# A four-layer graph network on one core: neighbour sums as DVE reduces, bias on POOL, residual on DVE, other orders, constant tiles on PE

## The chip, the cores and the metric

The kernel runs on one core of one Trainium2 chip. Its engines are PE (matrix multiply), DVE (vector), ACT (scalar and activation functions), POOL (here mainly the engine that issues indirect DMAs) and SP (plain DMAs); each runs its own stream in order, and they meet over semaphores. The metric is device time in microseconds (us) for one execution; the kernel before has a median of 1075.28 us over three runs (1071.92 to 1076.54).

## The reference

3327 nodes with 512 features each pass through four layers over one sparse adjacency matrix (int32, 3327 x 3327, each entry one with probability 0.0012, so about four neighbours a node). Each layer takes h = relu(layernorm(x)) and adds its result to x:

```python
# layer 0: mean over the neighbours, two linear maps, relu
deg = sum(mask); agg = mask @ h / max(deg, 1)
x = x + relu(concat([h @ W_self + b_self, agg @ W_nb + b_nb]) @ W_comb + b_comb)
# layers 1 (8 heads x 64), 2 (4 heads x 128, quaternion weights), 3 (1 head x 512)
Wh = h @ W
e = leaky_relu(f_src[n] + f_dst[m]); attn = softmax over the neighbours m of e
x = x + attn @ Wh            # layer 2: x + elu(attn @ Wh)
```

Only neighbours matter, so the sums over the matrix are sums over short lists.

## The kernel before

**Tiles, slots and units.** Nodes are sorted by their number of neighbours and cut into 26 tiles of 128. A tile has as many slots as its longest list: tile 0 has 14, tile 1 eight, tiles 2 and 3 seven, 4 to 6 six, 7 to 10 five, 11 to 15 four, 16 to 20 three, 21 to 23 two, 24 and 25 one: 117 slots. `ROWS` says how many nodes have a neighbour in each slot, in steps of 32; a tile's last slots can hold 96, 64 or 32 rows. One slot is one indirect DMA by POOL (L1562), which gathers one table row of some 2 KB per node into a ring of `RING` = 33 slots of 2080 bytes per partition. A unit is one tile or a pair of tiles worked together; `ORDERS` gives the units of each layer.

**Preparation.** The adjacency is loaded and turned into lists; x is normalised; folded weights are built; `keep_y` copies the own part of layer 0 (h times the own weights) from PSUM next to the node's x. Then `scatter` (L1435) writes 26 tiles of nodes' rows to their sorted places in DRAM, 26 indirect DMAs on POOL in the order `SEQUENCE`. `back` (L1451) reads the lists and degrees of all nodes back with one DMA on SP that waits for all scatters; `degrees` (L1505) turns them into `rdeg`, one over the degree. SP then loads x and own part of each tile (`xy`, L1854).

**Layer 0.** Per tile: gathers, a cast of the lists to integers (L1862), the sum over slots, x and output. PE sums most slots by multiplying with the identity into a PSUM tile `acc` (`sum_on_pe`, L1593); then DVE scales by `rdeg` and adds the own part (L1871), adds the bias (L1879), adds min(S//2, 5) further slots one at a time, each scaled (L1887), and makes the new x with relu and residual (L1895). `project` prepares the next layer's table: DVE statistics (L1649, L1650), ACT's logarithm and exponential for the inverse deviation (L822, L824) with small DVE operations (L831 to L836), ACT normalises (L1676), PE transposes into `pt` (L1694), ACT copies (L1705), PE multiplies by the weights into `pw` (L1780, L1737 for layer 3), ACT copies to `t` (L1803), and SP stores to the table (L1822).

**Layers 1 to 3.** `attend`: gathers; scores and softmax on DVE with the exponential on ACT (L1941 to L1978); products of rows and weights in place in the ring, some slots on ACT (L2096, as many as `ON_ACT` says), the others on DVE (L2110); sums on PE (L1593), in layer 1 also on DVE one slot at a time (L2138). Then the residual (L2148 in layer 1; an ELU, L2164 to L2178, in layer 2) and `project`. Layer 3 multiplies by its weights after the sum: the first slot on ACT (L2028), the others on DVE (L2030), transposes (L2046), copies (L2052), one identity matmul that puts the residual into `pw` (L2058) and four with the weights (L2060), a copy to `t` (L2067) and an indirect DMA on POOL that scatters the tile to the output (L2072).

**What sets the order.** Within the layers, `Plan` simulates the engines: each operation has a cost, a rank (layer, unit), what it waits for, and buffers that it takes and gives (`limits`: two `acc`, two `pt`, two `pw` and so on). The engines' streams are issued in the order of the simulated starts; the plan's times are not kept, only its order. Between layers, a small memset on POOL (`mark`, L2194) waits for the table stores, and the next layer's gathers stand behind it.

Of the kernel before, what the change touches and what calls it, by code (L numbers as in the profile page):

```python
# [8 lines left out]
F32 = mybir.dt.float32  # L9
# [9 lines left out]
P = 128  # L19
# [7 lines left out]
def general_path(  # L27
# [519 lines left out]
    def l3_finish(pc, i, o):  # L547
# [16 lines left out]
ROWS = (3328, 3072, 2592, 1984, 1344, 832, 448, 224, 128, 64, 32, 32, 32, 32, 0, 0)  # L564
CAPS = tuple(-(-r // 128) for r in ROWS)
SEG = 4
RING = 33
NEVER = -1.0e30
# [4 lines left out]
    0: {S: min(S // 2, 5) for S in range(1, SLOTS + 1)},  # L573
    1: {S: min(S // 2, 5) for S in range(1, SLOTS + 1)},
    2: {S: 0 for S in range(1, SLOTS + 1)},
# [4 lines left out]
        (24,), (12, 21), (11,), (6,), (18,), (17,), (15,), (4,), (3,), (20,), (5, 9), (22,), (10, 19), (1,),  # L580
        (2,), (14,), (0,), (23,), (8,), (13, 16), (7,), (25,),
    ),
    1: (
        (18, 21), (22, 24), (15,), (5,), (10, 20), (2,), (17,), (12, 23), (19,), (4,), (9, 14), (7,), (11, 16),
        (8, 13), (6,), (1,), (0,), (3,), (25,),
    ),
    2: (
        (18, 23), (19, 24), (16,), (20,), (6, 11), (10, 14), (7, 12), (5, 13), (9,), (1,), (21, 22), (4,), (0,),
        (8,), (2,), (3,), (15,), (17,), (25,),
    ),  # L590
    3: (
        (0,), (7,), (17,), (15, 20), (25,), (11,), (3,), (23,), (1, 5), (24,), (4, 14), (16,), (12, 22), (8,),
        (9,), (10,), (18,), (2,), (13,), (19,), (21,), (6,),
# [4 lines left out]
    1: {S: min(S // 3, 1) for S in range(1, SLOTS + 1)},  # L598
    2: {S: S // 5 for S in range(1, SLOTS + 1)},
}  # L600

SUMMED = {1: False, 2: False, 3: False}
# [11 lines left out]
class Plan:  # L614
# [35 lines left out]
    def run(self):  # L650
        free = {}
        stock = {tag: [0.0] * n for tag, n in self.limits.items()}
        waiting = {}
        for op in self.ops:
            if not op["need"]:
                waiting.setdefault(op["engine"], []).append(op)
        order = []
        while any(waiting.values()):
            best = None
            for engine, ops in waiting.items():  # L660
                for op in ops:
                    at = max(op["ready"], free.get(engine, 0.0))
                    for tag in op["take"]:
                        at = max(at, min(stock[tag])) if stock[tag] else None
                        if at is None:
                            break
                    if at is not None and (best is None or (at, op["rank"]) < best[:2]):
                        best = (at, op["rank"], op)
            at, _, op = best
            waiting[op["engine"]].remove(op)  # L670
            for tag in op["take"]:
                stock[tag].remove(min(stock[tag]))
            op["at"] = at
            end = at + op["cost"]
            free[op["engine"]] = end
            for tag in op["give"]:
                stock[tag].append(end + 0.1)
            for after in op["next"]:
                lag = op["lag"] + (0.1 if after["engine"] != op["engine"] else 0.0)
                after["ready"] = max(after["ready"], end + lag)  # L680
                after["need"] -= 1
                if not after["need"]:
                    waiting.setdefault(after["engine"], []).append(after)
            order.append((at, len(order), op))
        assert len(order) == len(self.ops)
        for _, _, op in sorted(order, key=lambda o: o[:2]):
            if op["emit"]:
                op["emit"]()
        return max(free.values())
# [3 lines left out]
def gnn_stack_kernel(  # L693
# [41 lines left out]
    with ExitStack() as st:  # L735
# [116 lines left out]
        with tc.tile_pool(name="p0", bufs=1) as pa, tc.tile_pool(name="p0p", bufs=2, space=PSUM) as pp:  # L852
# [444 lines left out]
            for p0 in range(0, NK, 2):  # L1297
# [25 lines left out]
                for j, i in enumerate(unit):  # L1323
# [51 lines left out]
                    own_done[i] = put("act", 0.62, late_rank, keep_y, (), [y], give=("py",))  # L1375
# [74 lines left out]
            def back():  # L1450
                ins = nc.sync.dma_start(srec_f, own.rearrange("(k p) w -> p k w", p=P)[:, :, 2 * D :])  # L1451
                for other in scattered:
                    tc.add_manual_dep(
                        ins.ins,
                        other.ins.name,
                        mybir.DependencyInfo(mybir.DependencyClass.Sync, mybir.DependencyReason.DATA),
                        reason="every row is read",
                    )
# [57 lines left out]
        with tc.tile_pool(name="run", bufs=1, reuse_waits="tile") as pr, tc.tile_pool(  # L1516
# [7 lines left out]
            limits = {"xy": 3, "acc": 2, "pt": 2, "pw": 2, "h": 3, "hT": 3, "t": 3, "neg": 2, "ee": 2, "y": 3}  # L1524
# [20 lines left out]
            def gather(layer, i, rank, barrier):  # L1545
# [8 lines left out]
                for s in range(S):  # L1554
# [16 lines left out]
                    landed.append(plan.add("dma", 0.95 * held(i, s) / P, rank, None, [issue], lag=1.3))  # L1571
                return ring[:, r0 : r0 + S, :], landed, last

            def runs_of(i, lo, hi, most=SLOTS):

                out = []
                for s in range(lo, hi):
                    if out and held(i, s) == out[-1][2] and s - out[-1][0] < most:
                        out[-1][1] = s + 1
                    else:  # L1580
                        out.append([s, s + 1, held(i, s)])
                return out

# [262 lines left out]
            for number, unit in enumerate(ORDERS[0]):  # L1846
                rank = (0, number)
                updated = []
                for j, i in enumerate(unit):
# [15 lines left out]
                    left = S - ON_DVE[0][S]  # L1865
                    summed = sum_on_pe(key, g, list(range(left)), [[o] for o in landed], rank)
# [9 lines left out]

                    def emit(key=key):
                        acc = tiles["acc", key]
                        nc.vector.tensor_tensor(acc, acc, biasf, ALU.add)  # L1879

                    done = plan.add("dve", 0.7, rank, emit, [done])
                    for s in range(left, S):

                        def emit(i=i, key=key, g=g, s=s):
                            m = held(i, s)
                            acc = tiles["acc", key][:m, :]
                            nc.vector.scalar_tensor_tensor(  # L1887
                                acc, g[:m, s, :D], rdeg[:m, i : i + 1], acc, ALU.mult, ALU.add
                            )

                        done = plan.add("dve", 0.7, rank, emit, [done, landed[s]])
                        last.append(done)

                    def emit(j=j, i=i, key=key, unit=unit):
# [11 lines left out]
                        plan.add("dve", 0.7 + 0.1 * SUMMED[1], rank, emit, [done], take=taking(1, j), give=("acc", "xy"))  # L1906
# [4 lines left out]
            def attend(layer, number, unit, barrier):  # L1911
# [12 lines left out]
                act_of = {i: ON_ACT[layer][slots_of[i]] if layer < 3 else 0 for i in unit}  # L1924
# [67 lines left out]
                for j, i in enumerate(unit):  # L1992
# [56 lines left out]
                    if layer == 3:  # L2049
# [6 lines left out]
                        def emit(i=i, key=key):  # L2056
                            pw = new("pw", key, [P, 2, D], pp)
                            nc.tensor.matmul(pw[:, 0, :], ident, xres[:, i, :], start=True, stop=False)  # L2058
                            for c in range(DC):
                                nc.tensor.matmul(  # L2060
                                    pw[:, 0, :], tiles["hT", key][:, c, :], w3[:, c, :], start=False, stop=(c == DC - 1)
                                )

                        done = plan.add("pe", 4.6, rank, emit, [turned], take=("pw",), give=("hT",))

                        def emit(key=key):
                            nc.scalar.copy(new("t", key, [P, WIDE])[:, :D], tiles["pw", key][:, 0, :])  # L2067

                        done = plan.add("act", 0.6, rank, emit, [done], take=("t",), give=("pw",))
# [18 lines left out]
                    else:  # L2088
# [38 lines left out]
                        left = Si - ON_DVE[layer][Si]  # L2127

                        first = sorted(range(left), key=lambda s: s < act_of[i])
                        summed = sum_on_pe(key, g[i], first, [[made[s]] for s in first], rank)  # L2130
                        last[i] += summed
                        done = summed[-1]
                        for s in range(left, Si):

                            def emit(i=i, key=key, s=s, g=g):
                                m = held(i, s)
                                acc = tiles["acc", key][:m, :]
                                nc.vector.tensor_tensor(acc, g[i][:m, s, :D], acc, ALU.add)  # L2138

                            done = plan.add("dve", 0.7, rank, emit, [done, made[s]])  # L2140
                            last[i].append(done)
                    if layer == 1:

                        def emit(j=j, i=i, key=key, g=g, Si=Si):
# [9 lines left out]
                                "dve", 0.7 + 0.1 * SUMMED[2], rank, emit, [done], take=taking(2, j), give=("acc",) if Si > 1 else ()  # L2154
# [4 lines left out]
                    else:  # L2159
# [10 lines left out]
                        def emit(j=j, i=i, key=key, g=g, Si=Si):  # L2170
# [6 lines left out]
                            else:  # L2177
# [4 lines left out]
                                "dve", 1.4 + 0.1 * SUMMED[3], rank, emit, [bent], take=taking(3, j), give=("acc", "ee") if Si > 1 else ("ee",)  # L2182
# [6 lines left out]
            for layer in (1, 2, 3):  # L2189
# [15 lines left out]
                ends = []  # L2205
                for number, unit in enumerate(ORDERS[layer]):
                    ends += attend(layer, number, unit, barrier)
            with tc.manual_schedule():
                plan.run()
# [50 lines left out]
```

## Time and profile before

| what | us |
|---|---|
| median of three runs | 1075.28 |
| the profiled execution, its span | 1230.0 |
| PE busy | 901.8 |
| DVE busy | 726.6 |
| POOL busy | 610.1 |
| ACT busy | 518.2 |
| preparation (to the first gather of layer 0) | 278 |
| layers 0, 1, 2, 3 (first gather to first gather, the last to its last issue) | 240, 245, 236, 219 |

The profile is one execution with records of every instruction; it took longer than the timed runs. Busy times of different engines overlap. A line of a group names source line, engine, operation, output and input, shape and count, then busy time and mean duration, then the idle time before it and what ended it. A line of a wait names who waited, for what, the total in us, how often, and the longest. The clock is the share of full speed that PE was granted.

### The profile page before, as it was taken

The page shows a single profiled execution, that of the slowest core. Times are in us where ns is not written, and L with a number is a line of the kernel's source. Part 1 is how long each engine was busy: PE and PEld are TensorE (multiplying, and loading weights), DVE is VectorE, ACT ScalarE, POOL GpSimd, SP SyncE. Part 2 cuts the span into 40 slices and gives each one's busy share as a digit, 9 for nine tenths or more (in the row PEclk, how much of TensorE's full clock was granted, in tenths as well). Part 3 has the DMA queues.
Part 4 walks back from the last instruction along what each step waited for, and adds up shares of the span by engine and source line. Part 5 has one row for each costly group of instructions (what it writes and reads, how often), then busy time and mean ns, then how long its engine had stood idle before and what let it go on. Part 6 is the DMA issues. An engine that isn't in the chain of part 4 may idle for free. (4 is left out here: it accounts for less than half of the span.)

```text
span 1230.0 us, 11605 instructions
## 1 busy us (share of the span) xinstructions
PE 901.8 (73%) x2853; PEld 510.4 (41%) x2853; DVE 726.6 (59%) x1848; ACT 518.2 (42%) x1700; POOL 610.1 (50%) x719
## 2 busy tenths in 40 slices
PE   7599999854098889752979796539979832948865
PEld 4244444322075656531647464214435421423322
DVE  6499989204176557453869784628894815534441
ACT  4488886210043433422656553316554621312221
POOL 1064246717655550175757511766883236675661
PEclk9899999977599899966989889659896956978987
DMA  9999894958587772265666521665754345575561
GB/s 352 338 364 338 294 306 146 317 203 286 172 268 252 247 249 89 76 195 149 198 183 178 154 79 55 189 187 150 209 169 129 91 121 149 168 206 160 163 186 59
DMA packets 89910, 240.49 MB, mean 196 GB/s; under 512 B 24933, under 2 KB 26477, under 8 KB 89834
## 3 DMA queue, kind: packets, MB, share of 16 engines
q0 software_dynamic: 41600, 137.72, 38.1%
q1 hardware_dynamic: 48234, 101.96, 23.3%
q8 instruction: 24, 0.39, 0.1%
q14 instruction: 52, 0.43, 0.1%
HBM read 190.35 MB, written 49.27 MB: 195 GB/s over the span
## 5 line engine op out<-in xcount | busy, mean ns | idle before, releaser
L1562 POOL DMA_INDIRECT ring<-table,nbr x351 | 368.5, 1050 | 185.5 <-issue 80.9
L1593 PE MATMUL acc<-ring,ident 128*128 128x512 f32 (+1 forms) x494 | 266.6, 676 | 66.8 <-DVE ring L2110 24.3
L1780 PE MATMUL pw<-w,hT 128*128 128x264 f32 (+1 forms) x832 | 197.3, 394 | 18.3 <-ACT hT L1705 13.6
L1780 PEld LDWEIGHTS pw<-w,hT 128*128 128x128 f32 x832 | 161.2, 195 | 60.9 <-ACT hT L1705 20.5
L1593 PEld LDWEIGHTS acc<-ring,ident 128*128 128x128 f32 (+1 forms) x494 | 98.7, 215 | 175.1 <-issue 107.5
L1562 POOL DMA_INDIRECT ring<-table,srec x117 | 110.1, 941 | 77.8 <-issue 31.5
L2110 DVE TENSOR_TENSOR ring<-ring,w 128x2048 f32<-128x2048 f32 (+7 forms) x76 | 114.3, 1531 | 4.7 <-DVE w L1978 3.0
L2060 PE MATMUL pw<-w,hT 128*128 128x512 f32 x208 | 101.7, 634 | 13.3 <-ACT hT L2052 11.0
L1209 DVE FIND_INDEX8 fidx<-one_i,ai 128x8 uint32<-128x832 int32 x104 | 104.2, 1018 | 0.0
L1349 PE MATMUL pz_n<-wf,hT_n 128*128 128x512 f32 x208 | 95.2, 609 | 10.9 <-ACT hT_n L1342 8.4
L1705 ACT ACTIVATE hT<-pt 128x128 f32<-128x128 f32 (+1 forms) x312 | 81.8, 292 | 39.7 <-PE pt L1694 18.5
L1217 ACT ACTIVATE junk<-ai 128x1664 int8<-128x1664 int32 (+1 forms) x52 | 82.7, 1590 | 32.6 <-DMA ai<-in_adj_dram 32.2
L1694 PE MATMUL pt<-ident,h 128*128 128x128 f32 x208 | 36.5, 312 | 75.9 <-ACT h L1676 73.4
L1349 PE MATMUL py_n<-wf,hT_n 128*128 128x512 f32 x208 | 91.9, 592 | 0.0
L1803 ACT COPY t<-pw 128x512 f32<-128x512 f32 (+1 forms) x54 | 30.6, 566 | 134.0 <-PE pw L1780 43.9
L1941 DVE TENSOR_TENSOR e<-ring,fs 128x24 f32<-128x24 f32 (+25 forms) x96 | 15.2, 172 | 120.2 <-DMA ring<-table,nbr 102.0
L2060 PEld LDWEIGHTS pw<-w,hT 128*128 128x128 f32 x208 | 42.3, 207 | 73.2 <-issue 51.3
L1705 ACT ACTIVATION_READ_ACCUMULATOR hT<-pt 128x1 f32 x312 | 69.5, 223 | 0.0
L1694 PEld LDWEIGHTS pt<-ident,h 128*128 128x128 f32 x208 | 28.1, 160 | 96.3 <-ACT h L1676 81.6
L2194 POOL MEMSET mark<- 1x1 f32 x3 | 0.3, 88 | 132.7 <-DMA table<-t 132.7
L1349 PEld LDWEIGHTS pz_n<-wf,hT_n 128*128 128x128 f32 x208 | 39.8, 195 | 62.8 <-issue 49.4
L2046 PE MATMUL pt<-ident,y 128*128 128x128 f32 x96 | 16.4, 312 | 67.4 <-issue 56.8
(185 smaller groups left out, 1319.7 us busy)
## 6 DMA issues: line engine op xcount, KB each, us to landing
ai<-in_adj_dram SPq DMA_DIRECT2D x25, 832.0 KB
ai<-in_adj_dram SPq DMA_DIRECT2D x25, 831.5 KB
table<-t SPq DMA_DIRECT2D x52, 258.0 KB
xy<-own SPq DMA_DIRECT2D x26, 512.0 KB
table<-t SPq DMA_DIRECT2D x26, 260.0 KB
table<-zt_n SPq DMA_DIRECT2D x26, 256.0 KB
ring<-table,nbr POOLq DMA_INDIRECT x351
later<-in_x_dram SPq DMA_DIRECT2D x15, 256.0 KB
```

The costliest lines, as they stand in the source:

```text
L1209: nc.vector.max_index(fidx[:, i, qq * 8 : (qq + 1) * 8], one_i, ai[:, q * QW : min(cols, (q + 1) * QW)])
L1217: nc.scalar.activation(junk[:, :cols], tiles["ai", key][:, :cols], AF.Square, accum_out=sq[:, i, hf : hf + 1])
L1349: nc.tensor.matmul(pz, tiles["hT", key][:, c, :], wf[s][:, c, :], start=(c == 0), stop=(c == DC - 1))
L1562: nc.gpsimd.indirect_dma_start(out=ring[:m, r0 + s, : width[layer]], out_offset=None, in_=table[layer], in_offset=bass.IndirectOffsetOnAxi ...
L1593: nc.tensor.matmul(acc, ident[:m, :], g[:m, s, :D], start=(k == 0), stop=(k == len(slots) - 1))
L1694: nc.tensor.transpose(pt[:, c, :], h[:, c * P : (c + 1) * P], ident)
L1705: nc.scalar.activation(hT[:, c, :n], pt[:, c, :n], AF.Copy, accum_out=hsum[layer][:, i, c : c + 1])
L1780: nc.tensor.matmul(pw[:, b, :w], tiles["hT", key][:, c, :], wsb[layer][:, c, b, :w], start=(c == 0), stop=(c == DC - 1),)
L1803: nc.scalar.copy(t[:, :D].rearrange("p (b f) -> p b f", b=2)[:, lo:hi, :], pw[:, lo:hi, :HD])
L2046: nc.tensor.transpose(pt[:, c, :], tiles["y", key][:, c * P : (c + 1) * P], ident)
L2060: nc.tensor.matmul(pw[:, 0, :], tiles["hT", key][:, c, :], w3[:, c, :], start=False, stop=(c == DC - 1))
L2110: nc.vector.tensor_tensor(v, v, box["w"][:m, j, lo:hi, :].unsqueeze(3).to_broadcast([m, hi - lo, H, O]), ALU.mult,)
```

## The change

- `ROWS` is rounded up to multiples of 128, so each gather takes full tiles of 128 rows. The number of gathers stays.
- `ON_DVE` now names tiles. Those named have all their slots summed by one DVE `tensor_reduce` over the slots into `acc`; the others are summed wholly on PE. Named are 22 tiles in layer 0 (111 slots), 12 in layer 1 (66 slots), four in layer 2 (15 slots). The slot-by-slot additions on DVE are gone.
- The bias of layer 0 is added on POOL, to the own part in preparation, ahead of the scatter.
- `back` reads the records with 26 DMAs on SP, one per tile, in layer 0's order of tiles.
- `SUMMED[2]`: the sums for the normalisation between layers 1 and 2 come from the residual operation's own row sum and from a square with row sum on ACT, in place of DVE's statistics. The code for this was there.
- In layer 3 the residual is added by DVE as it writes `t`; the identity matmul and ACT's copy are gone.
- `fill`: PE multiplies a constant bf16 tile of ones, 128 x 512, into a PSUM tile `warm` that nobody reads, wherever the plan sees PE idle, 3.6 times per idle microsecond: 776 in all. `pt` has one buffer in place of two, which makes room for `warm`.
- `ORDERS` and `ON_ACT` are other; `ON_ACT` is now per tile (layer 1: 13 slots on ACT in place of 21; layer 2: 30 in place of 12). The ring starts at slot 0 in each layer, and the plan's cost of a gather's landing is a constant.

```diff
-ROWS = (3328, 3072, 2592, 1984, 1344, 832, 448, 224, 128, 64, 32, 32, 32, 32, 0, 0)
+ROWS = (3328, 3072, 2688, 2048, 1408, 896, 512, 256, 128, 128, 128, 128, 128, 128, 0, 0)
+FILL = 3.6
 ON_DVE = {
-    0: {S: min(S // 2, 5) for S in range(1, SLOTS + 1)},
-    1: {S: min(S // 2, 5) for S in range(1, SLOTS + 1)},
-    2: {S: 0 for S in range(1, SLOTS + 1)},
+    0: frozenset((0, 1, 2, 3, 4, 5, 6, 7, 8, 9, 10, 11, 12, 13, 14, 15, 16, 17, 18, 19, 20, 23,)),
+    1: frozenset((0, 2, 3, 4, 6, 7, 10, 13, 14, 16, 19, 23,)),
+    2: frozenset((3, 16, 17, 22,)),
 }
...
-    1: {S: min(S // 3, 1) for S in range(1, SLOTS + 1)},
-    2: {S: S // 5 for S in range(1, SLOTS + 1)},
+    1: (1, 1, 1, 1, 0, 0, 2, 1, 0, 1, 2, 0, 1, 1, 1, 0, 0, 0, 0, 0, 0, 0, 0, 0, 0, 0),
+    2: (5, 4, 1, 1, 0, 0, 1, 0, 1, 2, 0, 3, 1, 1, 1, 1, 1, 2, 1, 1, 0, 1, 1, 1, 0, 0),
 }
-SUMMED = {1: False, 2: False, 3: False}
+SUMMED = {1: False, 2: True, 3: False}
...
+        until = 0.0
+        for at, _, op in sorted(order, key=lambda o: o[:2]):
+            if op["engine"] == "pe" and fill:
+                for _ in range(int((at - until) * FILL)):
+                    fill()
+                until = at + op["cost"]
...
+                    o = put("act", 0.62, late_rank, keep_y, (), [y], give=("py",))
+                    def add_bias(i=i):
+                        own = node(i)[:, D : 2 * D]
+                        nc.gpsimd.tensor_tensor(own, own, biasf, ALU.add)
+                    own_done[i] = put("pool", 1.28, late_rank, add_bias, (), [o, whole])
...
-                ins = nc.sync.dma_start(srec_f, own.rearrange("(k p) w -> p k w", p=P)[:, :, 2 * D :])
+                for k in (k for unit in ORDERS[0] for k in unit):
+                    ins = nc.sync.dma_start(srec_f[:, k, :], own[k * P : (k + 1) * P, 2 * D :])
...
+            warm = pp.tile([P, DC, P], F32, tag="warm", name="warm", bufs=1)
+            def fill():
+                nc.tensor.matmul(
+                    warm, ones16, ones16.unsqueeze(1).to_broadcast([P, DC, P]), start=True, stop=True
+                )
-            limits = {"xy": 3, "acc": 2, "pt": 2, "pw": 2, ...
+            limits = {"xy": 3, "acc": 2, "pt": 1, "pw": 2, ...
...
+            def sum_on_dve(key, g, S, needs, rank):
+                def emit():
+                    nc.vector.tensor_reduce(
+                        new("acc", key, [P, D], pp), g[:, :S, :D].rearrange("p s d -> p d s"), AX.X, ALU.add
+                    )
+                return [plan.add("dve", 0.1 + 0.535 * S, rank, emit, needs, take=("acc",))]
...
-                    def emit(key=key):
-                        acc = tiles["acc", key]
-                        nc.vector.tensor_tensor(acc, acc, biasf, ALU.add)
-                    for s in range(left, S):
-                        def emit(i=i, key=key, g=g, s=s):
-                            nc.vector.scalar_tensor_tensor(
-                                acc, g[:m, s, :D], rdeg[:m, i : i + 1], acc, ALU.mult, ALU.add
-                            )
...
-                            nc.tensor.matmul(pw[:, 0, :], ident, xres[:, i, :], start=True, stop=False)
...
-                            nc.scalar.copy(new("t", key, [P, WIDE])[:, :D], tiles["pw", key][:, 0, :])
+                            nc.vector.tensor_tensor(
+                                new("t", key, [P, WIDE])[:, :D], tiles["pw", key][:, 0, :], xres[:, i, :], ALU.add
+                            )
```

## The prediction

> **What bounds the kernel now.** I read the clock and span first, then busy time by stage, then the waits of each stage, then the prices of single instructions. The stages are cut where POOL starts the first gather of a layer: preparation to 278 us, layers 0 to 3 from 278, 518, 763 and 999 us. Columns of the stage table: busy us (instructions) of PE, PEld, DVE, ACT, POOL, then clock, DMA share, GB/s.
>
> ```profile
> core 0: 1230.0 us, clock 0.855
> ...
> 278.00:518.00 240.00, 174.71 (x654) 119.23 (x654) 130.56 (x305) 78.27 (x359) 110.22 (x118) 0.88 0.64 206
> 518.00:763.00 245.00, 180.79 (x650) 121.69 (x650) 165.93 (x397) 119.27 (x539) 124.02 (x118) 0.85 0.51 149
> 763.00:999.00 236.00, 171.87 (x546) 93.58 (x546) 151.47 (x374) 109.69 (x443) 134.12 (x118) 0.78 0.53 154
> 999.00:1218.00 219.00, 140.40 (x364) 65.50 (x364) 91.37 (x252) 47.59 (x96) 135.87 (x143) 0.81 0.56 164
> ```
>
> PE is the busiest engine in layers 0 to 2, DVE is close behind it in 1 and 2. In layer 3 it is POOL: besides 136 us busy it has about 0.3 us of issue between its 143 transfers (43 us), 179 of 219 us. The waits of layer 0, then those of the whole run:
>
> ```profile
> POOL mark L2194 <- DMA table<-t: 56.1, 1, 56.1
> DVE acc L1871 <- remote: 42.5, 2, 36.1
> PE pt L1694 <- ACT h L1676: 37.6, 2, 36.6
> ...
> ACT t L1803 <- PE pw L1780: 28.9, 13, 4.8
> ```
>
> ```profile
> POOL mark L2194 <- DMA table<-t: 132.7, 3, 56.1
> ...
> DVE e L1941 <- DMA ring<-table,nbr: 102.0, 19, 20.7
> ...
> POOL out_dram L2072 <- ACT t L2067: 37.1, 10, 5.9
> ```
>
> POOL has issued its gathers long before a layer ends (it waits 133 us at the three marks), so PE, DVE and ACT set the length of layers 0 to 2. The single waits of 36.1 and 36.6 us on DVE and PE are one standstill of all three engines while POOL issues the first gathers of the layer; the timeline shows the like in layers 1 to 3 (about 18, 20 and 35 us). This execution is 1230 us long, the median is 1075.28: a ratio of 0.874. Most of the 155 us can lie in these 110 us of standstill, so I count them as unchanged. I make the sum on 1230 us and scale by 0.874.
>
> The prices that carry the rest, by shape (count | busy, mean ns | idle before):
>
> ```profile
> L1593 PE MATMUL acc<-ring,ident 128*128 128x512 f32 x472 | 254.0, 675 | 66.7 <-DVE ring L2110 24.3 <-issue 22.6 <-DMA ring<-table,srec 15.3
> ...
> L2058 PE MATMUL pw<-xres,ident 128*128 128x512 f32 x52 | 31.1, 685 | 0.3 <-ACT t L2067 0.3
> ```
>
> ```profile
> L1879 DVE TENSOR_TENSOR acc<-acc,biasf 128x512 f32<-128x512 f32 x26 | 18.1, 698 | 0.7
> ...
> L1148 DVE TENSOR_REDUCE w<-later 128x8 f32<-128x512 f32 x8 | 5.1, 667 | 0.0
> ...
> L1423 DVE TENSOR_REDUCE rank<-ai_sort 128x26 f32<-128x416 f32 x1 | 1.0, 951 | 0.0
> ...
> L1975 DVE TENSOR_REDUCE den<-ex 128x8 f32<-128x24 f32 x3 | 0.5, 159 | 0.3 <-ACT ex L1968 0.3
> ...
> L1975 DVE TENSOR_REDUCE den<-ex 128x8 f32<-128x56 f32 x2 | 0.5, 234 | 0.0
> ...
> L1975 DVE TENSOR_REDUCE den<-ex 128x8 f32<-128x112 f32 x1 | 0.3, 323 | 0.0
> ```
>
> **The price of the new sum.** The new reduce adds S slots that lie 2080 bytes apart, so neighbours in the sum are never neighbours in memory. L1148 reduces contiguous data: 667 ns for 512, about 1.05 ns an element over a fixed 0.13 us. L1975 is a strided sum like the new one. From 56 to 112 elements (7 and 14 per output) it grows by 89 ns: 1.59 ns an element over 0.145 us. With 3 per output it takes 159 ns for 24, no dearer than contiguous. L1423, 16 per output, is the dearest: (951-156)/416 = 1.91, or 2.29 with its fixed part. I take 1.59 for tiles of four slots or more, 1.05 below, and keep 1.05 and 1.91 as ends. The Trainium skill ("VectorE: DVE Perf Modes", the perf-mode tier table and the advice at its end) gives this instruction only the 1x rate and says to restructure where it is on a hot path; at that rate a slot would be about 0.54 us (an estimate), the low end here, and layer 0 would gain 28 us. The strided rows exceed it, in the direction of "SBUF — State Buffer" on 16-byte lines; no row has this stride.
>
> **Layer 0: -2 us.** DVE loses 50 multiply-adds (L1887, 50 x 0.753 = 37.6), 26 bias adds (18.1) and eight casts (1.4). It gains 22 reduces: 94 slots in tiles of four or more, 94 x 512 x 1.59 = 76.5; 17 others, 9.1; fixed 3.2; together 88.8. 130.6 becomes 162.3, with some 13 us of gaps between instructions 175. PE loses 61 of its 67 slots at 0.86 warm, 52 us: DVE becomes the bound. First multiply-add at 288 (below), 288 + 175 = 463, the same tail as now (last L1871 at 500.0 and two more to 502.2, next layer at 518.6: 16.4), plus the standstill 36.6: 516 against 518.6. At 1.05 DVE drops 26 us more: -28, and POOL's 146 us of issue is the next limit. At 1.91: +13.
>
> **Layer 1: -4 us.** DVE loses 50 adds (L2138, 34.6), the statistics for layer 2 (17.9 + 4.7) and some 1.5 of short operations. It gains 12 reduces (58 slots at 1.59: 47.2; 8 at 1.05: 4.3; fixed 1.7), 4.5 for eight slots' products from ACT, 3.0 for 19 small operations and perhaps 2.6 for the row sums: 166 becomes 171. PE has 66 slots to lose and 50 to take over: -13.8, to 167. ACT: -16 for products, +27 for 26 squares at 0.82 (row of L1676) and 0.22 to read the sum: 130. The longest engine falls from 181 to 171; half of that reaches the end, as PE and DVE wait for each other in turn. Ends -10 and +5.
>
> **Layer 2: -6 us.** 15 slots leave PE, 13 us off its 172, the longest. DVE stays (+11 for reduces, -10 for 18 slots' products), ACT rises by 23 to 133. ACT stands between PE's sum and the ELU, so I take half; ends -13 and +3.
>
> **Layer 3: -9 us.** PE loses the residual's 52 passes (0.86 warm a tile), ACT its copy (584 ns), DVE gains an add (691): each tile's chain to the output scatter is 0.75 us shorter. POOL stood 10 times for this chain, and gathers queue behind it: -7. The last unit has 3 slots for 6: -2. DVE's 18 us stand beside 128 idle us. Ends 0 and -25, if most of the 37 us of waits went.
>
> **Head: +3 us.** 26 adds of 1.28 us (row of L1131, 1278 ns) go to POOL, nine of them among the scatters that end preparation: the last waits for ACT's copy and puts +1.3 to +3.2 before the last scatter. The records' read-back (L1451) becomes 26 issues of 0.37 us on SP: 9.6 us. The first gather needs only the first and starts about 1 us earlier; but the degrees need all, and the loads of own parts queue behind on SP, so the first multiply-add comes at 288 instead of 284.8, and the reduces behind it on DVE with it. Ends +1 and +5.
>
> **Fillers: -4 us.** 776 multiplies of constants go into PE's stream where the plan sees PE idle (195, 127, 184, 270 by layer). At 0.22 to 0.43 us (nearest: 128x264 and 128x512 passes) they take 171 us or more. PE is idle 272 us in these stages now, about 162 without the standstills, and loses 101 of work: it fits, in program order, not by the clock. What they can win is the half clock: 0.78 means 104 us at half speed in layer 2. PE is no longer the sole bound, so -4; ends -14 and +15. The Trainium skill ("TensorE: Matmul & The Clock Gate", the HAM clock gate) lets the clock fall after an idle window of about 3.4 us, and by it constant work would hold it near full; the trace's 0.78 to 0.88 agrees in kind, and the sum by the page would be the -14 end.
>
> **At nothing or little.** One transpose buffer for two: the next tile's transposes wait for four copies on ACT, which four pw groups mostly cover: +1, at most +6. Full rows in all gathers: the issue price is the same and the DMA share is 0.51 to 0.64, which covers 1.7 MB more a layer: 0, at most +4. The new orders are in the terms above.
>
> **Sum.** -2 -4 -6 -9 +3 -4 +1 = -21: 1209 us, times 0.874 = 1057.
>
> **Rivals.** *The strided reduce is dearer* and makes DVE the bound of layers 0 and 1. Each 0.1 ns costs 4.8 us in layer 0 and about 1.5 in layer 1; the gain of 21 is gone at 1.92 ns. For: L1423. Against: the L1975 rows. At 2.29: 1230 - 21 + 44 = 1253, that is 1095. *It runs like contiguous data* (L1148): -28 and -10 in place of -2 and -4: 1177, 1029. *The gains turn into waits*: POOL's issue and the marks hold, layers 0 to 2 stay, layer 3 gives 4, the head takes 3: 1229, 1074. *Fillers on the path*: a quarter of 171 us in front of real work, +43 for -4: 1256, 1098; against it stand PE's idle rows.
>
> **How the numbers follow.** Forecast 0.41; dear reduce 0.22; cheap reduce 0.17; gains hidden 0.11; fillers 0.09. A measurement of this kernel tells about 0.5% (5 us) from no change. Faster takes the forecast but 0.02 and the cheap reduce, with a little of the hidden case: 0.57; same 0.10; slower 0.33. All ends together give 998 and 1120; 1012 to 1104 leaves out 2 in 10. The forecast's own range is 1040 to 1068.
>
> **What would show it.** The reduce's rows: 14 slots 11.5 us by my price, 7.7 by the cheap one. DVE busy 162 us in layer 0 with PE near 110 apart from fillers; the clock above 0.9; waits on L2072's successor below 30 us; degrees read at 285. I am wrong if the reduce is off by 0.3 ns, or if PE's waits sit behind fillers.

## The result

The changed kernel is slower: 1116.02 us (median of four; 1110.77 to 1116.54) against 1075.91, a ratio of 1.036, 95% interval [1.0326, 1.0395]. A second set of runs gave 1.0387 [1.0333, 1.0441] (e14).

The profile of before that the prediction reads spans 1230.0 us, though the executions timed with it took 1072 to 1077, and in the two sets of runs of e5 to e12 the kernel before takes about 1236 us; in all other sets it takes 1074 to 1076 and its second profile (e1) spans 1068.8, so sizes are compared within these alone.

The profiles of before (e1) and after, by stage: bounds and length, then busy us of PE, PEld, DVE, ACT and POOL, then clock, DMA share and GB/s. First before:

```profile
core 0: 1068.8 us, clock 0.901
...
265.75:450.65 184.90, 168.98 (x654) 116.20 (x654) 130.77 (x305) 78.41 (x359) 110.28 (x119) 0.96 0.80 267
450.65:653.93 203.28, 168.43 (x650) 115.43 (x650) 164.97 (x397) 118.70 (x539) 128.04 (x118) 0.94 0.62 179
653.93:865.36 211.43, 171.01 (x546) 91.63 (x546) 150.81 (x374) 110.27 (x443) 140.19 (x118) 0.81 0.59 171
865.36:1068.80 203.44, 135.46 (x364) 63.03 (x364) 91.71 (x252) 47.32 (x96) 136.75 (x143) 0.82 0.61 178
```

Then after:

```profile
core 0: 1114.7 us, clock 0.933
...
274.15:485.37 211.22, 169.13 (x731) 117.24 (x732) 171.10 (x241) 77.11 (x357) 110.74 (x118) 0.91 0.73 246
485.37:707.32 221.95, 189.50 (x748) 125.93 (x747) 173.75 (x327) 123.15 (x526) 137.44 (x118) 0.92 0.61 172
707.32:908.54 201.22, 178.02 (x703) 97.09 (x702) 149.33 (x343) 131.61 (x511) 130.91 (x118) 0.92 0.66 189
908.54:1114.70 206.16, 167.16 (x562) 75.17 (x560) 106.22 (x264) 34.77 (x70) 137.51 (x143) 0.94 0.64 184
```

Of the 46 us between the two spans, preparation has 8, layer 0 has 26, layer 1 has 19, layer 3 has 3; layer 2 gives 10 back. PE's busy time now includes 198 us of constant multiplies.

In layer 0 DVE is busy 171 of 211 us, and 168 of the 177 us from its first scaling with the degrees (289.8) to its last residual (466.8). The reduces of after, by shape (elements read; count | busy, mean ns | idle before):

```profile
L1607 DVE TENSOR_REDUCE acc<-ring 128x512 f32<-128x3584 f32 x5 | 32.9, 6588 | 0.1
...
L1607 DVE TENSOR_REDUCE acc<-ring 128x512 f32<-128x7168 f32 x2 | 26.2, 13085 | 0.1
L1607 DVE TENSOR_REDUCE acc<-ring 128x512 f32<-128x2048 f32 x7 | 25.5, 3650 | 0.0
L1607 DVE TENSOR_REDUCE acc<-ring 128x512 f32<-128x1536 f32 x9 | 17.3, 1920 | 0.0
```

From 7 to 14 slots a reduce grows by 6497 ns: 928 ns a slot, 1.81 ns an element, against 640 ns a slot in a tile of three. The waits of layer 0 say what that does:

```profile
ACT ln L828 <- DVE mv L1679: 74.2, 16, 28.5
POOL mark L2201 <- issue: 48.9, 1, 48.9
ACT h L1705 <- DVE nmr L842: 35.3, 19, 5.1
...
DVE degs L1518 <- DMA srec<-own: 25.7, 1, 25.7
```

ACT stands 74 us for a tile's statistics (40.8 in e1), since the next tiles' reduces stand before them on DVE, and POOL, with all gathers out, waits 49 us at the mark that ends the layer (34.9 in e1). DVE itself waited until 288.4 for the degrees; in e1 it had them at 265.0. Its reading of the degrees and its first scaling (start, us, engine, line), in e1:

```profile
264.95 0.18 DVE L1505 CAST degs<-srec 128x26 f32<-128x26 int32 x1 [11.15 <-DMA srec<-own]
272.82 0.76 DVE L1871 SCALAR_TENSOR_TENSOR acc<-acc,rdeg,xy 128x512 f32<-128x512 f32 x1 [1.98 <-PE acc L1593]
```

and after:

```profile
288.37 0.18 DVE L1518 CAST degs<-srec 128x26 f32<-128x26 int32 x1 [25.70 <-DMA srec<-own]
289.83 0.76 DVE L1902 SCALAR_TENSOR_TENSOR acc<-acc,rdeg,xy 128x512 f32<-128x512 f32 x1 [0.91 <-DMA xy<-own]
```

From the first scaling to the first gather of layer 1 it is 177.8 us in e1 and 195.6 after. So layer 0 ends 35 us later: 17 because its first scaling comes later, 18 because the stretch behind it is longer.

### The profile page after: what moved, and what is told of

The parts are those of the page before. It is cut to its first block, busy times and chain, and to the rows that moved or that the text cites. A ratio compares the mean times of both kernels' runs of the same rounds, so it can differ in the third digit from the quotient of the medians.

```text
span 1114.7 us, 12395 instructions
## 1 busy us (share of the span) xinstructions
PE 942.1 (85%) x3393; PEld 527.9 (47%) x3393; DVE 796.5 (71%) x1693; ACT 529.8 (48%) x1727; POOL 652.0 (58%) x745
## 5 line engine op out<-in xcount | busy, mean ns | idle before, releaser
L1582 POOL DMA_INDIRECT ring<-table,nbr x351 | 379.3, 1080 | 124.0 <-issue 82.6
L1540 PE MATMUL warm<-ones 128*128 128x512 bf16 x776 | 198.0, 400 | 0.0
L1622 PE MATMUL acc<-ring,ident 128*128 128x512 f32 x310 | 158.3, 648 | 22.2 <-DMA ring<-table,srec 12.1
L1607 DVE TENSOR_REDUCE acc<-ring 128x512 f32<-128x1536 f32 (+7 forms) x38 | 170.0, 4472 | 0.5
L1540 PEld LDWEIGHTS <-ones 128*128 128x128 bf16 x776 | 79.3, 103 | 88.2 <-issue 22.4
L2125 DVE TENSOR_TENSOR ring<-ring,w 128x2048 f32<-128x2048 f32 (+3 forms) x66 | 108.2, 1664 | 1.5
L1223 ACT ACTIVATE junk<-ai 128x1664 int8<-128x1664 int32 (+1 forms) x52 | 82.8, 1592 | 35.1 <-DMA ai<-in_adj_dram 34.9
L1622 PEld LDWEIGHTS acc<-ring,ident 128*128 128x128 f32 x310 | 58.8, 204 | 81.6 <-issue 47.0
L1355 PE MATMUL py_n<-wf,hT_n 128*128 128x512 f32 x208 | 95.3, 610 | 0.0
L1955 DVE TENSOR_TENSOR e<-ring,fs 128x16 f32<-128x16 f32 (+15 forms) x72 | 12.6, 179 | 76.0 <-DMA ring<-table,nbr 75.4
L1705 ACT ACTIVATE h<-xres,nmr,rs 128x512 f32<-128x512 f32 x52 | 41.5, 818 | 53.3 <-DVE nmr L842 35.3
```

The lines of the kernel that those rows point to most:

```text
L1223: nc.scalar.activation(junk[:, :cols], tiles["ai", key][:, :cols], AF.Square, accum_out=sq[:, i, hf : hf + 1])
L1355: nc.tensor.matmul(pz, tiles["hT", key][:, c, :], wf[s][:, c, :], start=(c == 0), stop=(c == DC - 1))
L1540: nc.tensor.matmul(warm, ones16, ones16.unsqueeze(1).to_broadcast([P, DC, P]), start=True, stop=True)
L1582: nc.gpsimd.indirect_dma_start(out=ring[:m, r0 + s, : width[layer]], out_offset=None, in_=table[layer], in_offset=bass.IndirectOffsetOnAxi ...
L1607: nc.vector.tensor_reduce(new("acc", key, [P, D], pp), g[:, :S, :D].rearrange("p s d -> p d s"), AX.X, ALU.add)
L1622: nc.tensor.matmul(acc, ident[:m, :], g[:m, s, :D], start=(k == 0), stop=(k == len(slots) - 1))
```

## The experiments

Layer lengths in us, from the profiles of the sets in which the kernel before takes 1074 to 1076 (stages cut as above):

| kernel | median | prep. | L0 | L1 | L2 | L3 |
|---|---|---|---|---|---|---|
| before (e1) | 1072.3 | 265.8 | 184.9 | 203.3 | 211.4 | 203.4 |
| after | 1116.0 | 274.1 | 211.2 | 222.0 | 201.2 | 206.2 |
| e2, after without constant multiplies | 1125.6 | 272.1 | 212.4 | 223.0 | 202.8 | 215.7 |
| e3, after with the old split of sums | 1091.2 | 269.9 | 192.4 | 219.1 | 201.7 | 207.8 |
| e4, after with pair additions | 1089.5 | 274.8 | 190.5 | 218.5 | 196.7 | 207.9 |
| e13, before with the reduces alone | 1165.1 | 266.5 | 222.8 | 234.3 | 226.6 | 208.6 |
| e14, after again | 1120.1 | 270.8 | 211.2 | 224.3 | 204.0 | 206.9 |
| e15, before with layer 2's order and ACT slots | 1068.7 | 266.0 | 184.5 | 204.8 | 203.1 | 202.6 |
| e16, e15 with weights in PSUM | 1077.8 | 267.3 | 189.4 | 212.4 | 198.3 | 202.9 |
| e17, before with one transpose buffer | 1093.4 | 268.8 | 190.0 | 215.7 | 218.3 | 203.4 |
| e18, e15 with more ACT slots in layer 1 | 1079.4 | 265.4 | 183.7 | 217.8 | 203.4 | 205.2 |

A profiled span differs from the median of its kernel by up to 8 us, and preparation by up to 5 us between profiles that share it.

**e1, the kernel before again.**

> The kernel before, unchanged, for a second profile of it. Both theories: 1076 us, no difference. Theory of the profiling artefact: the standstills of 18 to 37 us at the start of each layer belong to the first profiled execution, not to the kernel; a second profile then has a span near 1075 us and layers of about 200 us. If they belong to the kernel, the span is near 1230 again.

1072.34 us, ratio 0.9987 [0.9955, 1.0019], span 1068.8. PE, DVE and ACT are idle together for 5, 9, 10.5 and 26 us of layers 0 to 3, against 48, 25, 25 and 37 in the first profile: most of the standstills are not the kernel's, save in layer 3. What is left in each layer is one run of gathers and a tail. POOL issues layer 0's 117 gathers in 145.5 us without one wait, layer 1's in 163.3, layer 2's in 175.4, and layer 3's in 176.6, with the output scatters and 13.1 us of waits for their tile between them. Behind its last gather it waits 34.9, 35.8 and 35.2 us at the marks (the tail, below), and layer 3 lasts another 26.8. So POOL's issue is the longest single stretch of every layer, which the first profile hid. PE is still the busiest engine (169 of 185 us in layer 0).

**e2, no constant multiplies.**

```diff
-                plan.run(fill)
+                plan.run()
```

> The changed kernel without the 776 constant multiplies on PE. Theory 1 (the strided sums on DVE, 0.93 us a slot, bound layers 0 and 1): 1105 to 1125 us against 1116, since DVE stays saturated; PE's clock falls from 0.93. Theory 2 (the constant multiplies stand in front of real work on PE): 1085 us or less.

1125.57 us, 1.0512 [1.0478, 1.0546], at the upper end of theory 1 and 5 to 10 us slower than with them (1116 and, in e14, 1120), and the clock falls from 0.933 to 0.864. Theory 2 is out: the constant multiplies help. Nearly all of it is in layer 3 (215.7 against 206.2), where the clock goes from 0.94 to 0.80; layers 0 to 2 differ by 1 to 2 us.

**e3, the old split of the sums.**

```diff
-                    if i in ON_DVE[0]:
-                        summed = sum_on_dve(key, g, S, landed, rank)
-                    else:
-                        summed = sum_on_pe(key, g, list(range(S)), ...)
+                    left = S - min(S // 2, 5)
+                    summed = sum_on_pe(key, g, list(range(left)), ...)
+                    (then one scalar_tensor_tensor a slot, as before; tensor_tensor in layer 1; layer 2 wholly on PE)
```

> The changed kernel with the sums split as before (up to five slots a tile one at a time on DVE in layers 0 and 1, the rest on PE, layer 2 wholly on PE), all else changed. Theory 1: DVE falls by some 66 us in layer 0 and 26 in layer 1 and the time to 1060 to 1085 us. Theory 2, or a loss in the preparation, the orders or the row sums: it stays above 1100 us.

1091.18 us, 1.0183 [1.0148, 1.0219]: 25 us of the loss go, 19 of them in layer 0. The expected range was missed by 6 us at the upper end: 17 us stay. Layer 1 is 16 us longer than before and layer 0 7.5, layer 2 gives 10 back, so the reduces are not all of it. From the first scaling (286.0) to layer 1 it is 176.3 us, as in e1 (177.8): what is left of layer 0's loss lies ahead of the first scaling.

**e4, pair additions.** The same slots on DVE, summed by contiguous additions of halves:

```diff
-                    nc.vector.tensor_reduce(new("acc", ...), g[:, :S, :D].rearrange("p s d -> p d s"), AX.X, ALU.add)
+                    n = S
+                    while n > 2:
+                        h = n // 2
+                        nc.vector.tensor_tensor(g[:, :h, :D], g[:, :h, :D], g[:, n - h : n, :D], ALU.add)
+                        n -= h
+                    nc.vector.tensor_tensor(new("acc", ...), g[:, 0, :D], g[:, 1, :D], ALU.add)
```

> The changed kernel with the same slots on DVE, but each reduce replaced by contiguous additions of halves in the ring (14 slots: 7, 3, 2 and the last pair into PSUM). By the row of the products (1215 ns for 1024 elements) a tile costs about (S-1) x 0.53 + 0.14 us an addition: layer 0's sums fall from 104 to about 56 us, layer 1's from 60 to 33. Theory 1 (the price of the strided read is what costs): 1050 to 1085 us. Theory 2 (something else in the change): 1100 us or more.

1089.48 us, 1.0164 [1.0122, 1.0205], between the two ranges expected. DVE's busy time in layer 0 falls from 171.1 to 128.9, so the same sums cost 42 us less there as contiguous additions: the strided read is the price. Layer 0 falls by 21. Layer 1 falls by 3.5 only, though DVE is busy 148 us there in place of 174. But POOL's gathers in layer 0, never held up before, now take 161.7 us in place of 155.8 although they wait for no ring slot any more, and the mean issue goes from 946 to 1080 ns:

```profile
L1582 POOL DMA_INDIRECT ring<-table,srec x117 | 126.4, 1080 | 41.3 <-issue 31.1 <-DMA srec<-own 6.3 <-DMA ring<-table,srec 1.5
```

**e5 to e8, three undos and a part.** The before of this set takes 1236.43 us.

```diff
e5: -SUMMED = {1: False, 2: True, 3: False}
e5: +SUMMED = {1: False, 2: False, 3: False}
e6:  ORDERS and ON_ACT as before
e7:  back() with one DMA, no add_bias on POOL, the bias added on DVE in layer 0
e8:  before, with ROWS, ON_DVE and sum_on_dve of the changed kernel
```

e5 to e7 are made from e4.

> The kernel with pair additions (1089 us), with DVE's statistics for layer 2 as before (no squares on ACT, no row sums). Its layer 1 took 218 us against 203 before. If the squares on ACT lengthen the chain from a tile's residual to its transposes, layer 1 falls by 8 to 15 us: 1074 to 1082. If the orders or the slots per engine do it: 1085 to 1100, since DVE gets 23 us more.

> The kernel with pair additions, with the units' orders and the slots on ACT of before in all layers. If the orders cost layer 1 its 15 us, the time falls to 1070 to 1080, and layer 2 (197 us against 211 before) shows whether its gain came from them too (then it gives back 10). If the orders do nothing: 1089 within 5.

> The kernel with pair additions, with the records read back by one DMA and the bias added on DVE in layer 0. In the changed kernel the first gather starts at 274 us against 266 and the first scaling with the degrees at 289.8. If this head is a loss: first gather near 267, preparation and layer 0 together 6 to 10 us shorter, 1080 to 1084. If it is covered: 1089 or more, as DVE gets 18 us more in layer 0.

> The kernel before with only the sums changed: full rows in the gathers and the strided reduces of the same tiles (111, 66 and 15 slots) in place of DVE's additions one at a time. If the reduces' price decides: layer 0 goes from 185 to 210 us (DVE near 195 busy, bias still on it), layer 1 from 203 to 210, 1100 to 1120 in all. If the sums only cost together with the new orders and the rest: 1070 to 1085.

Ratios to their own before: e5 1.0116 [1.0051, 1.0181], e6 1.035 [1.0281, 1.0418], e7 1.0122 [1.0079, 1.0166], e8 1.0315 [1.0221, 1.041]. e4 was not run beside them, so e5 and e7 decide nothing on the row sums and the head; the first gather of e7 starts at 276.4 us, not near 267. Within the set e6 is 30 us slower than e5 and e7, so going back to the old orders and slots does not seem to help there. e8 was repeated (e13).

**e9 to e12, the weights in PSUM, and the old head once more** (before: 1235.7 us).

```diff
+            wps = pp.tile([P, D], F32, tag="wps", name="wps", bufs=1)
...
+                            wp = wps[:, at : at + n * S * H]        # at = 0, 128, 256, 384 in turn
+                            nc.vector.tensor_tensor(wp, ex, den.unsqueeze(2)..., ALU.mult)
...
-                                    box["w"][:m, j, lo:hi, :].unsqueeze(3).to_broadcast(...)
+                                    box["wp"][:m, j, lo:hi, :].unsqueeze(3).to_broadcast(...)
```

e9 is this in the kernel before, with one transpose buffer to make room; e11 in the changed kernel without constant multiplies and their PSUM tile; e12 in e3 without them; e10 is e7 again.

> The kernel before with the softmax weights that DVE multiplies by also written to PSUM, so that these products (L2110) have one operand in the ring and one in PSUM (one transpose buffer, to make room). In the second profile of before 15 gathers of layer 1 are 0.7 to 1.7 us longer than the others (17 us in all, 30 in layer 2), and each ends just after a product on DVE ends. Theory A (such a product with both operands in SBUF holds up POOL's issue): the long gathers vanish, the gathers of layer 1 take 146 to 150 us in place of 163, of layer 2 in place of 176, and the time falls by 10 to 45 us. Theory B (the long gathers come from the DMA queues): they stay, and the time is that of before within 8 us.

> The kernel with pair additions, the records read back by one DMA and the bias added on DVE in layer 0, beside runs of the kernel before that are like those of the first experiments. If the new head is a loss: first gather near 267 us in place of 274, total 6 to 10 us less than the 1089 of the pair additions. If it is covered by DVE's 18 us more: 1089 within 5.

> The changed kernel without the constant multiplies and with the softmax weights in PSUM. In the changed kernel layer 1 took 222 us against 203; its gathers 173 against 163, 26 us of that in long ones. If POOL's hold-ups make layer 1's loss: layer 1 falls to 205 or less. If DVE's work makes it (174 us busy): the gathers get shorter, the tail behind them longer, and the layer stays above 215.

> The changed kernel with the sums split as before, no constant multiplies, and the softmax weights in PSUM: with the gathers' hold-ups gone and DVE not the bound, 1045 to 1075 us, under both kernels. If the constant multiplies or something else is needed: 1090 or more.

Ratios: e9 1.0419 [1.0368, 1.0471], e10 1.0156 [1.0094, 1.0217], e11 1.02 [1.0112, 1.0288], e12 1.0222 [1.0184, 1.026]. In e9, e11 and e12 the long gathers are gone (theory A on the cause): what issues take beyond the usual 0.95 us sums to under 0.5 us a layer. But the time did not follow: all three are slower than their before. In these runs POOL waits for ring slots instead, 35 to 67 us in each of layers 0 to 2 (28 to 42 in the first profile of before). In e10 the first gather starts at 278.3 us, not near 267. e16 asks for the weights in PSUM again, beside a before of 1075.79 us.

**e13 and e14, the reduces alone, beside the changed kernel.** e13 is e8, e14 the changed kernel.

> The kernel before with only the sums changed (full rows, strided reduces of the same tiles), again, beside the changed kernel. If the reduces make most of the loss: 25 to 45 us over before. If POOL's longer gathers, the head and the orders make it: under 15 us.

> The changed kernel once more, beside the same runs of before as the other three: 3 to 5% over before; less than 2% if the loss belongs to the runs in which it was first timed.

e13: 1165.11 us, 1.0832 [1.0787, 1.0878]; e14: 1120.09, 1.0387. The reduces alone cost 90 us, twice the upper end expected and twice what the whole change costs:

```profile
266.47:489.23 222.76, 140.95 (x532) 108.08 (x532) 189.51 (x269) 78.31 (x359) 110.75 (x118) 0.81 0.69 230
```

DVE is busy 190 of layer 0's 223 us, since here the bias is still on it. Beside the reduces the other parts of the change win 45 us back; beside the old sums (e3) they lose 17. Which of them win was not tried apart; the bias alone takes 18 us off DVE in layer 0.

**e15, layer 2's settings alone.**

```diff
-        (18, 23), (19, 24), (16,), (20,), (6, 11), (10, 14), ...      (ORDERS[2])
+        (24,), (19,), (18,), (22,), (16,), (17, 21), (8, 23), ...
-    2: {S: S // 5 for S in range(1, SLOTS + 1)},                      (ON_ACT)
+    2: (5, 4, 1, 1, 0, 0, 1, 0, 1, 2, 0, 3, 1, 1, 1, 1, 1, 2, 1, 1, 0, 1, 1, 1, 0, 0),
```

> The kernel before with only layer 2's order of units and its slots on ACT from the changed kernel. Layer 2 took 211 us before and 201 after; its long gathers (POOL held up) came to 30 us before and 20 after. If the 18 products fewer on DVE make that gain: layer 2 shorter by 7 to 12 us, the time 0.6 to 1.1% below before. If the gain needs the row sums, the constant multiplies or the reduces: no change within 0.3%.

1068.73 us, 0.9934 [0.9908, 0.996], as expected: 0.7% under before and 4.6% under the changed kernel beside it (e14). Layer 2 is 8 us shorter. Its gathers take 167.2 us in place of 175.5, the long ones 21 in place of 30, with DVE's busy time there 10 us less. Order and slots on ACT were changed together; which of them does how much was not tried apart.

**e16, and the weights in PSUM.**

> The same with the softmax weights in PSUM in layers 1 and 2 (one transpose buffer). The long gathers vanish in both layers. Where a layer's gathers and the work behind them set its length, 15 to 40 us less than before; if the layers are bound by PE or by the landing of the data, no gain or a loss, as in e9 (1.042).

1077.82 us, 1.0011 [0.9991, 1.0032]: no gain. The gathers behave as expected; of layers 1 and 2, and of the groups:

```profile
456.74:669.12 212.38, 170.33 (x650) 117.08 (x650) 167.15 (x414) 118.30 (x539) 110.25 (x118) 0.93 0.60 172
669.12:867.43 198.31, 158.68 (x546) 86.43 (x546) 141.45 (x373) 130.82 (x511) 110.50 (x119) 0.84 0.63 183
```

```profile
L1564 POOL DMA_INDIRECT ring<-table,nbr x351 | 331.2, 944 | 134.6 <-issue 59.1 <-DMA table<-t 19.5 <-DMA ring<-table,nbr 13.1
```

The mean issue is 944 ns (1079 in e1), layer 2's gathers take 145.7 us in place of 167.2 in e15, and the tail behind them grows from 29.4 to 46.1: 17 of the 21 us come back. In layer 1 the gathers take 154.5 and the tail 51.3. So POOL's issue alone does not set the length of these layers. But e16 also has one transpose buffer, needed for room, and that alone costs 19 us (e17); what the weights in PSUM win beside two buffers is open.

**e17, one transpose buffer.**

```diff
-            limits = {"xy": 3, "acc": 2, "pt": 2, ...
+            limits = {"xy": 3, "acc": 2, "pt": 1, ...
```

> The kernel before with one transpose buffer instead of two and nothing else. By layer 0 of e16: the tail behind the last gather 2 us longer and the restart 2 us longer, in each of the three layer boundaries: 8 to 15 us over before. If the buffer costs nothing and e16's 4.5 us came from elsewhere: within 3 us.

1093.4 us, 1.0173 [1.0147, 1.02]: some 19 us, more than expected. Layers 0 to 2 are 5, 12 and 7 us longer. The end of layer 0 shows how. PE's and ACT's operations in e1 (start, us, engine, line; "x8" is two tiles):

```profile
438.21 1.04 PE L1694 MATMUL pt<-ident,h 128*128 128x128 f32 x8
438.41 0.58 ACT L1803 COPY t<-pw 128x512 f32<-128x512 f32 x1 [0.52 <-PE pw L1780]
439.45 7.39 PE L1780 MATMUL pw<-w,hT 128*128 128x264 f32 x32 [0.20 <-ACT hT L1705]
```

and in e17:

```profile
444.02 0.60 PE L1694 MATMUL pt<-ident,h 128*128 128x128 f32 x4
444.23 0.59 ACT L1803 COPY t<-pw 128x512 f32<-128x512 f32 x1 [4.13 <-PE pw L1780]
445.27 3.83 PE L1780 MATMUL pw<-w,hT 128*128 128x264 f32 x16 [0.64 <-ACT hT L1705]
448.93 0.60 PE L1694 MATMUL pt<-ident,h 128*128 128x128 f32 x4
```

With two buffers PE transposes two tiles and then multiplies for both in one block of 32 passes, while ACT copies the second. With one, each tile is transposed alone, ACT first writes the previous tile's table row and then the copies, and PE waits: 4.9 us a tile, where two tiles took 8.6.

**e18, more products of layer 1 on ACT.**

```diff
-    1: {S: min(S // 3, 1) for S in range(1, SLOTS + 1)},
+    1: {S: min(S // 3, 2) for S in range(1, SLOTS + 1)},
```

> e15 (layer 2's order and slots on ACT from the changed kernel) with up to two slots a tile on ACT in layer 1 as well (28 in place of 21). If DVE's products holding up POOL are what layer 1 can still lose: its long gathers fall from 17 to about 13 us and the time to 1062 to 1067. If ACT's eight activations a slot (2.2 us) come onto the chain: 1068 to 1080.

1079.4 us, 1.0051 [1.003, 1.0072], 11 us more than e15, in the second theory's range: layer 1 goes from 204.8 to 217.8, its gathers stay near 165 and the tail grows from 36.6 to 48.4, with ACT busy 132 us there in place of 119 and DVE 161 in place of 165. That ACT's activations come onto the chain fits this; the chain itself was not followed.

## Why the prediction was wrong

The forecast of 1057 missed by 59 us and had the wrong sign. The step that failed by most is layer 0, forecast at -2 and measured at +26: its reference, a layer of 240 us less one standstill, was too long, and the later first scaling was mis-sized. Next comes layer 1, forecast at -4 and measured at +19, where the single transpose buffer, put at +1 for the whole kernel, alone costs 12. The rival that ends slower, the dear reduce, was right in place and effect, but its own sum does not give the loss: at the measured 1.81 ns an element (1.59 taken, 1.92 named as the point where the gain is gone) the prediction's own rates (4.8 and 1.5 us for each 0.1 ns) bring its sum from -21 to -7, still faster.

- *Standstill.* This step failed. "I count them as unchanged" left the layer of before too long. From the first scaling to layer 1 the prediction has 197 us before without the standstill (518.6 - 36.6 - 284.8) and 191 after (175 + 16.4). Measured are 177.8 and 195.6: after is right within 4 us, before 19 us too long, so a gain of 6 was forecast where 18 are lost. e3 has 176.3 there, so the 18 are the reduces'. That after fits so well is in part luck: DVE is busy 168 us in the stretch where 162.3 was predicted, and its gaps are 9 us, not 13.
- *What bounds the kernel.* "PE, DVE and ACT set the length of layers 0 to 2" was read from a profile in which POOL waits inside the layers, and holds only in part. In e1 POOL's gathers run without a break for 145 to 175 us of these layers' 185 to 211, while PE is busy 168 to 171. Neither is the sole bound: e16 takes 21 us off layer 2's gathers (with one transpose buffer) and the layer falls by 5. That work taken off PE had little to win, since POOL's run stays, is likely but was not tried alone.
- *Layer 0's price.* The reduces were priced at 1.59; at 1.81 they are 10 us dearer, and DVE is busy 171.1 in the layer where 162.3 was predicted. e13 and e4 show that it is the strided read. The Trainium skill ("VectorE: DVE Perf Modes", the perf-mode tier table) gives the 1x rate, by which a slot would be 0.54 us (an estimate); measured are 0.93, and 0.64 with three. The runs show the dear side; that the 16-byte lines of "SBUF — State Buffer" (Specifications) are the reason was not tried apart.
- *Head, +3.* Mis-sized: the first scaling is 17 us later. The last scatter starts at 267.2 in place of 254.7, with bias additions among the scatters. In the first profile the scatters waited 16.6 us for ACT's copies, which seemed to cover the additions; in e1 these waits are 3.7 us. Reading back in 26 parts lets the first gather start 6.9 us after the last scatter in place of 11.1, but the degrees come 21.2 us after it in place of 10.2. No run beside a before of 1074 to 1076 us undoes the head alone, but the first scaling comes at 272.5 to 275.9 in the six profiles there with the old head (e1, e13, e15 to e18) and at 286.0 to 290.7 in the five with the new one (after, e2 to e4, e14).
- *Layer 1, -4.* Measured +19. DVE's busy time was predicted well (171, measured 173.8), but the gathers take 172.7 in place of 163.3, long issues 26 in place of 17, and the tail 42.7 in place of 35.8. The reduces make little of it here: with DVE busy 150 (e3) and 148 (e4) the layer still takes 219. One transpose buffer alone makes +12 (e17). The reduces alone make +31 in the kernel before (e13), where DVE is busy 189 us.
- *Layer 2, -6.* Measured -10, and by luck: the prediction took it from PE's 13 us; e15 gets 8 us of it with order and slots on ACT alone, without moving a sum off PE.
- *Layer 3, -9.* Measured +3. POOL's 37 us of waits for the output tile belonged to the execution of 1230 us; e1 has 13.1, after 10.2, and the run of gathers and scatters stays (176.6 and 177.4 us).
- *Fillers, -4.* Right in sign, 5 to 10 us in size (e2), nearly all in layer 3.
- *One transpose buffer, +1, at most +6.* The term that was mis-sized by the largest factor: +19 alone, in the kernel before (e17). "Which four pw groups mostly cover" had the order on PE wrong: the next tile's transposes stand behind the previous tile's multiplies, and its own multiplies wait for its copies. The 17 us that e3 leaves are about this size; but no run gives the changed kernel its second buffer back, so that they are the buffer's is not shown.

## What to carry to other kernels

If a profiled execution is 14% longer than the timed ones, its waits need not be the kernel's: take another profile before pricing anything, above all before naming the bound. A strided reduce with four or more distant rows is dearer than its element count: the same sum by contiguous halves took 42 us less of DVE in one layer. A second buffer between two engines that alternate can be worth more than it looks: giving it up cost the kernel before 19 us (e17), more than the filler that took its place brought the changed one (5 to 10, e2).

## What the runs showed beside

POOL's issue of an indirect DMA is held up when it begins during a DVE operation with two operands in SBUF. In e1 (start, us, engine, line):

```profile
537.20 0.94 POOL L1562 DMA_INDIRECT ring<-table,nbr  x1 [0.30 <-DVE rs L834]
537.32 2.28 DVE L2110 TENSOR_TENSOR ring<-ring,w 128x2048 f32<-128x2048 f32 x1
538.45 1.96 POOL L1562 DMA_INDIRECT ring<-table,nbr  x1 [0.30 <-issue]
```

The second gather begins while the product runs and ends 0.8 us after it, 1.96 us in place of 0.95; the first, begun 0.12 us before the product, is not held up. All 42 gathers of layers 1 and 2 of e1 that take over 1.15 us begin inside such a product (15 more begin so and are not long). In e16, where one operand is in PSUM, 64 begin inside a product and one of them is long. Such gathers cost 17 us in layer 1 and 30 in layer 2 of e1; with one operand in PSUM they are gone, but for one a layer at most (e9, e11, e12, e16), with one transpose buffer alone they stay (e17: 24 and 30), and pair additions in the ring bring 15 us of them into layer 0 (e4). The reduces hold nothing up: layer 0 of after has none.

The Trainium skill ("SBUF — State Buffer", Who interferes with whom) says that a DVE operation with two SBUF inputs contends with a GpSimd instruction that reads SBUF. It also reports that such an operation did not stall a DMA, and infers the reason from descriptor generation; for these indirect DMAs, which read their row numbers from the tile `nbr`, the runs show that it does, and the measurement decides. Which read is held up was not tried. The skill's statement that a reduce never contends on this chip agrees with layer 0 of after, where an issue takes 946 ns on average.
